# A channel gate behind a ConvNeXt block: two small layers as single-column products, or one product with a matrix of ones

## The chip, the cores and the metric

The kernel runs on one core of a Trainium2 chip. The metric is the device time of one execution in microseconds, from runs of the same program on a chip. The profile is of one further execution, so its own time is named wherever a sum is made from it. The engines are TensorE (PE in the profile, its weight loads PEld), VectorE (DVE), ScalarE (ACT), GpSimd (POOL) and SyncE (SP), whose queue here only starts transfers.

## What is computed

There are 32 samples of 384 channels and 28 x 28 places, all in f32. Layer 0 is a ConvNeXt block with a response normalization; layer 1 is a gate over channels, made from three statistics of each channel.

```python
# layer 0
y = conv7x7_depthwise(x)                       # per channel
y = (y - mean_c) * rsqrt(var_c + 1e-6)         # over channels, at each place
y = gelu(y @ w1 + b1)                          # 384 -> 1536
gx = sqrt(sum over places of y**2)
y = grn_g * (y * gx / (mean(gx) + 1e-6)) + grn_b + y
x = x + (y @ w2 + b2)                          # 1536 -> 384
# layer 1, R = 8
avg, mx, mn = mean, max, min of x over places  # each (32, 384)
avg_out = avg @ W1.T
max_out = einsum('brg,rg->br', mx.reshape(b, 8, 48), W2_1) * W2_2
min_out = mn @ W3.T
logits = concat([avg_out, max_out, min_out]) @ Wfc.T     # 24 -> 384
out = sigmoid(logits + x)
```

The last lines are the gate's two layers: 24 numbers a sample out of 3 x 384 statistics, and 384 logits out of the 24 numbers. A logit is added to every place of its channel.

## The kernel before

**Stage one (L175 to about L403).** The depthwise convolution of all samples runs as products with banded matrices. Four matrices (tmat, L203) are in flight; they are read from a table in DRAM that is built at the start from the filter weights (dww, L156). The input is loaded in 96 tiles (xi, L227), padded by GpSimd (xpad, L237), transposed by TensorE (pt, L248), and moved to SBUF by VectorE and ScalarE. There are 48 steps over the channels, eight a step (the loop at L315), each with three products a channel (L344, L345, L348). GpSimd also combines the weights of both dense layers in this stage (form_w, L268), because the dense layers use sums of blocks of weights, fewer products than the plain layer has; SyncE stores each combination (L277) in DRAM. The small constants are loaded in this stage too, one a step (the dictionary `later`).

**Stage two.** A loop over the samples runs up(b + 1), the first dense layer, and then down(b), the second. The rest of the work on other samples is hung between the steps of down as hooks (beside): the normalization of sample b + 2 (turn, stats, std), the forms of its input (forms_up, L542, ten GpSimd additions a sample), the scaling of sample b + 1 (grn and scale), and the gate of sample b - 1 (gate_store at hook 9, or hook 7 for the last). down has 15 steps of four products (L673) with 392 columns each. Each step's result is added to the residual x by VectorE (L687, L689). The last addition into a half of a channel block also sums it (accum_out into `sh`), and once both halves of a block are done VectorE takes its maximum and minimum over the places (L694, L695, into `st`). The operands of down are forms of y, made by GpSimd (forms, L648): seven are asked for at the last hook of the sample before (d_p, d_q, one in place, d_r, d_s, d_t, d_u) and three in down itself (d_v, and two written in place into y).

**The gate.** gate_store (from L701) runs 12 products of one column each into one bank: the six half sums, the three maxima and the three minima, each against a 128 x 24 matrix `gate` (L709). VectorE copies the 24 sums (comb, L714). Three products of one column with the 24 x 128 blocks of Wfc follow (pl, L717), and VectorE copies the logits (lg, L721). ScalarE adds them inside the sigmoid (L723), and its queue stores the sample (L729). The matrix `gate` is written between the stages in the code (L423 to L442).

**What sets the order.** The kernel is recorded by a layer that keeps tiles and their waits. It places each engine's instructions by when it reckons that they can run, so the order in an engine's queue need not be that of the code: the constants of the gate are written after stage one in the code, but their instructions stand in the queues among those of stage one. On an engine the queue runs in order. A pool with one buffer (psum `small`: pg, pa and pl share one bank) makes the next user wait for the last reader.

Of the kernel before, what the change touches and what calls it, by code (L numbers as in the profile page):

```python
# [8 lines left out]
F32 = mybir.dt.float32  # L9
AF = mybir.ActivationFunctionType  # L10
ALU = mybir.AluOpType
AX = mybir.AxisListType

P = 128
C = 384
CB = C // P
FF = 4 * C
FB = FF // P
HW = 28
NT = HW * HW  # L20
NH = NT // 2
RH = HW // 2
R = 8
EPS = 1e-6
# [95 lines left out]
def convnext_gate_kernel(  # L120
# [13 lines left out]
    nc = tc.nc  # L134
# [3 lines left out]
    const = ctx.enter_context(tc.tile_pool(name="const", bufs=1))  # L138
    dram = ctx.enter_context(tc.tile_pool(name="dram", bufs=1, space=bass.MemoryType.DRAM))
    smp = ctx.enter_context(tc.tile_pool(name="smp", bufs=3))  # L140
    pss = ctx.enter_context(tc.tile_pool(name="pss", bufs=1, space=bass.MemoryType.PSUM))

    def small(name):
        return pss.tile([P, 512], F32, tag="small", name=name)
# [7 lines left out]
    yl = dram.tile([P, NLAST, B, NJ * YC], F32, name="yl")  # L152


    dww = const.tile([P, CB, 49], F32, name="dww")
    nc.sync.dma_start(dww, dw_w.rearrange("(cb p) t -> p cb t", p=P))  # L156
    ident = const.tile([P, P], F32, name="ident")
    make_identity(nc, ident)
    cv = const.tile([P, 5, CB], F32, name="cv")
    _, lng_t, lnb_t, b2_t, w21_t = (cv[:, i, :] for i in range(5))  # L160
    fv = const.tile([P, 3, FB], F32, name="fv")
    b1_t, gg_t, gb_t = (fv[:, i, :] for i in range(3))
    ones_f = const.tile([P, P], F32, name="ones_f")
    nc.gpsimd.memset(ones_f, 1.0 / FF)
    awt = const.tile([P, 2, CB, R], F32, name="awt")
    w22b = const.tile([P, R], F32, name="w22b")
    wfc = const.tile([3 * R, C], F32, name="wfc")
    eps_t = const.tile([P, 1], F32, name="eps_t")
    nc.gpsimd.memset(eps_t, EPS)

# [4 lines left out]
    with ExitStack() as one:  # L175
        tp = one.enter_context(tc.tile_pool(name="tp", bufs=1))
# [5 lines left out]
        psc = one.enter_context(tc.tile_pool(name="psc", bufs=4, space=bass.MemoryType.PSUM))  # L182

        ws = tp.tile([P, CB * FF], F32, name="ws")
        tab = tp.tile([P, CB, FL], F32, name="tab")
        dwb = tp.tile([P, C], F32, name="dwb")


        NT2 = 4
# [74 lines left out]
        w1v = ws.rearrange("p (k t m c) -> p t k m c", t=KT, m=3, c=P)  # L264
        w2v = ws.rearrange("p (t k m c) -> p t k m c", t=KT, k=3, c=P)
        U1, U2 = 4, 22

        def form_w(name, wv, text, dst):  # L268

            t = ufp.tile([P, KT, P], F32, tag="uf", name=name)  # L270
            for n, (sg, m, k) in enumerate(terms(text)):
                blk = wv[:, :, int(k), m, :]
                if n == 0:
                    nc.gpsimd.tensor_scalar(t, blk, float(sg), None, ALU.mult)
                else:
                    nc.gpsimd.tensor_tensor(t, t, blk, ALU.add if sg > 0 else ALU.subtract)
            nc.sync.dma_start(dst, t)  # L277

        AHEAD = 6
        for i in range(AHEAD):  # L280
# [1 line left out]
        xt = new_xt(0)  # L282
# [32 lines left out]
        for s in range(NK):  # L315
# [8 lines left out]
            if s in later:  # L324

                dst, src = later[s]
# [11 lines left out]
            t = tmat[s % NT2]  # L338
# [56 lines left out]
                        nc.vector.bn_stats(bs0[:, j, 0, :], yi[:, : NY - NLAST, j, :])  # L395
            if si == SK - 1:
                xt = xn
            i = s - U1
            if 0 <= i < NS:
                form_w(f"u1_{i}", w1v, UPSTEPS[i][1], u1d[:, :, i, :].rearrange("t p c -> p t c"))  # L400
# [16 lines left out]

    def bank(name):
        return psz.tile([P, 512], F32, tag="pz", name=name)

    gate = const.tile([P, 3, CB, 3 * R], F32, name="gate")  # L423
    nc.vector.memset(gate, 0.0)
    nc.vector.tensor_scalar(gate[:, 0, :, 0:R], awt[:, 0], 1.0 / NT, None, ALU.mult)
    nc.vector.tensor_copy(gate[:, 2, :, 2 * R : 3 * R], awt[:, 1])
    grp = const.tile([P, CB, R], F32, name="grp")
    for cb in range(CB):
        nc.vector.tensor_scalar(grp[:, cb, :], w22b, w21_t[:, cb : cb + 1], None, ALU.mult)

    G = C // R
    grp_a = const.tile([P, CB, R], F32, name="grp_a")
    nc.gpsimd.affine_select(
        out=grp_a, in_=grp, pattern=[[P, CB], [-G, R]], compare_op=ALU.is_ge,
        fill=0.0, base=0, channel_multiplier=1,
    )
    grp_b = const.tile([P, CB, R], F32, name="grp_b")
    nc.gpsimd.affine_select(
        out=grp_b, in_=grp_a, pattern=[[-P, CB], [G, R]], compare_op=ALU.is_ge,
        fill=0.0, base=G - 1, channel_multiplier=-1,  # L440
    )
    nc.vector.tensor_copy(gate[:, 1, :, R : 2 * R], grp_b)  # L442


    x_tiles, yts, sts, accs, pts, feats = {}, {}, {}, {}, {}, {}
# [156 lines left out]
    def grn(b):  # L602

        ssq = ssqs.pop(b)
        gx = smp.tile([P, FB], F32, tag="gx", name=f"gx_{b}")
        nc.scalar.activation(gx, ssq, AF.Sqrt)
        gs = smp.tile([P, 1], F32, tag="gs", name=f"gs_{b}")
        nc.vector.tensor_reduce(gs, gx, AX.X, ALU.add)
        pg = small(f"pg_{b}")
        nc.tensor.matmul(pg[:, 0:1], ones_f, gs, start=True, stop=True)  # L610
        ge = smp.tile([P, 1], F32, tag="ge", name=f"ge_{b}")
        nc.vector.tensor_scalar(ge, pg[:, 0:1], EPS, None, ALU.add)
        gr = smp.tile([P, 1], F32, tag="gr", name=f"gr_{b}")
        nc.vector.reciprocal(gr, ge)
        gn = smp.tile([P, FB], F32, tag="gn", name=f"gn_{b}")
        nc.vector.scalar_tensor_tensor(gn, gx, gr, gg_t, ALU.mult, ALU.mult)
        gsc = gscs[b] = smp.tile([P, FB], F32, tag="gsc", name=f"gsc_{b}")
        nc.vector.tensor_scalar(gsc, gn, 1.0, None, ALU.add)  # L618
# [32 lines left out]
    def down(b, hooks):  # L651

        xt = x_tiles.pop(b)
        o = ops[b]
        st = smp.tile([P, 2, CB], F32, tag="st", name=f"st_{b}")
        sh = smp.tile([P, CB, 2], F32, tag="sh", name=f"sh_{b}")
        left = {}
        for step in STEPS:
            for _, m, h in terms(step[4]):
                left[m, h] = left.get((m, h), 0) + 1  # L660
        made = EARLY
        banks = {}
        for i, (opnd, _, bk, first, reads) in enumerate(STEPS):
            while opnd not in o:
                forms(b, made, made + 1)
                made += 1
            wt = up2.tile([P, KT, P], F32, tag="u2", name=f"u2_{b}_{i}")
            nc.sync.dma_start(wt.rearrange("p t c -> p (t c)"), u2d[i])
            if first:
                banks[bk] = bank(f"pz_{b}_{bk}")  # L670
            pz = banks[bk]
            for t in range(KT):
                nc.tensor.matmul(  # L673
                    pz[:, :NH],
                    wt[:, t, :],
                    o[opnd][:, t, :],
                    start=(first == 1 and t == 0),
                    stop=(t == KT - 1),
                    skip_group_check=True,
                )  # L680
            for sg, m, hn in terms(reads):
                h = "ab".index(hn)
                xh = xt[:, m, h * NH : (h + 1) * NH]
                op = ALU.add if sg > 0 else ALU.subtract
                left[m, hn] -= 1
                if left[m, hn]:
                    nc.vector.tensor_tensor(xh, xh, pz[:, :NH], op)  # L687
                    continue
                nc.vector.scalar_tensor_tensor(  # L689
                    xh, xh, b2_t[:, m : m + 1], pz[:, :NH], ALU.add, op,  # L690
                    accum_out=sh[:, m, h : h + 1],
                )
                if not left[m, "ab"[1 - h]]:
                    nc.vector.tensor_reduce(st[:, 0, m : m + 1], xt[:, m, :], AX.X, ALU.max)  # L694
                    nc.vector.tensor_reduce(st[:, 1, m : m + 1], xt[:, m, :], AX.X, ALU.min)  # L695
            run(hooks, i)
        ys.pop(b)
        ops.pop(b)
        gates[b] = xt, st, sh

    def gate_store(b):  # L701

        xt, st, sh = gates.pop(b)
        ov = out[b].rearrange("(cb p) n -> p cb n", p=P)
        pa = small(f"pa_{b}")
        cols = [(0, cb, sh[:, cb, h : h + 1]) for cb in range(CB) for h in range(2)]
        cols += [(v, cb, st[:, v - 1, cb : cb + 1]) for v in (1, 2) for cb in range(CB)]
        for n, (v, cb, col) in enumerate(cols):
            nc.tensor.matmul(  # L709
                pa[: 3 * R, 0:1], gate[:, v, cb, :], col,  # L710
                start=(n == 0), stop=(n == len(cols) - 1),
            )
        comb = smp.tile([3 * R, 1], F32, tag="comb", name=f"comb_{b}")
        nc.vector.tensor_copy(comb, pa[: 3 * R, 0:1])  # L714
        pl = small(f"pl_{b}")
        for cb in range(CB):
            nc.tensor.matmul(  # L717
                pl[:, cb : cb + 1], wfc[:, cb * P : (cb + 1) * P], comb, start=True, stop=True
            )
        lg = smp.tile([P, CB], F32, tag="lg", name=f"lg_{b}")  # L720
        nc.vector.tensor_copy(lg, pl[:, :CB])  # L721
        for cb in range(CB):
            nc.scalar.activation(  # L723
                xt[:, cb, :], xt[:, cb, :], AF.Sigmoid, bias=lg[:, cb : cb + 1], scale=1.0
            )
            if b == B - 1:
                nc.sync.dma_start(ov[:, cb, :], xt[:, cb, :])
        if b < B - 1:
            nc.scalar.dma_start(ov, xt)  # L729
# [138 lines left out]
```

## Time and profile before

| what | value |
|---|---|
| median of three runs | 3219.02 us (3218.94 to 3219.2) |
| the profiled execution, its own time | 3216.78 us |
| its span, first to last instruction | 3215.1 us, granted clock 0.996 |
| TensorE busy | 3174.8 us (99%) |
| VectorE, ScalarE, GpSimd busy | 1669.3, 1886.1, 1607.1 us |
| a sample in the steady stretch (pa to pa) | 84.19 us |
| end of stage one's last product | about 496.2 us |

The span is the time between the first and the last instruction of the profiled execution; 1.7 us of its own time lie around it. "Busy" means that an instruction of the engine was under way. A row of a timeline has the start in us, the duration in us, the engine, the line, the operation, the operands with their shapes, and the number of instructions merged into the row; a note in brackets gives the idle time of that engine just before and what ended it. One f32 product leaves two matmul records and two weight loads. A row of several merged products starts with the first and ends with the last, and since the products are pipelined, the distance from the start of one row to the start of the next is what a row costs.

### The profile page before, as it was taken

How to read it: one execution, taken by the hardware profiler on the slowest of the kernel's cores; microseconds unless marked ns; L12 is line 12 of the kernel's file. 1: busy time of each engine (PE TensorE's matmuls, PEld its weight loads, DVE VectorE, ACT ScalarE, POOL GpSimd, SP SyncE). 2: the span in 40 equal slices, each digit the busy share in tenths (PEclk: the TensorE clock that was granted, in tenths of full speed). 3: DMA queues.
4: the chain of work that ended last, by engine and by line, in shares of the span. 5: the costliest groups of instructions: out<-in, count | busy, mean ns of one | idle time of the engine just before them, and what ended most of it. 6: DMA issues, size and time to landing. Idle time of an engine off the chain costs nothing.

```text
span 3215.1 us, 35678 instructions
## 1 busy us (share of the span) xinstructions
PE 3174.8 (99%) x12352; PEld 2009.1 (62%) x12352; DVE 1669.3 (52%) x3442; ACT 1886.1 (59%) x3032; POOL 1607.1 (50%) x821
## 2 busy tenths in 40 slices
PE   8999998999999999999999999999999999999998
PEld 7999995555555555555555555555555555555555
DVE  3443436555555555555555555555555555555553
ACT  2222225766666666666666666666666666666662
POOL 2453511645555555555555555555555555555554
PEclk9999999999999999999999999999999999999999
DMA  9999985444444444344444444444444444444333
GB/s 346 364 340 359 341 296 183 131 131 136 130 139 143 141 141 139 132 136 143 134 142 145 134 145 143 136 140 139 146 146 129 137 129 141 142 141 141 125 101 126
DMA packets 257160, 540.84 MB, mean 168 GB/s; under 512 B 121021, under 2 KB 130774, under 8 KB 247766
## 3 DMA queue, kind: packets, MB, share of 16 engines
q1 hardware_dynamic: 244148, 500.70, 46.1%
q10 hardware_dynamic: 12834, 37.88, 3.5%
q8 instruction: 98, 1.61, 0.2%
q14 instruction: 80, 0.66, 0.1%
HBM read 447.53 MB, written 90.99 MB: 167 GB/s over the span
## 4 chain that ended last, share of the span: by engine, by line
PE 98%; DVE 1%; ACT 1%; DMA 1%; issue 0%; SPq 0%; ACTq 0%; POOL 0%; DVEq 0%; POOLq 0%
PE ph_A L576 14%; PE ph_B L576 13%; PE pz_A L673 11%; PE pz_B L673 10%; PE pz_C L673 5%; PE pz_E L673 5%; PE ph_C L576 5%; PE pc L344 5%; PE pc L345 4%; PE pc L348 4%; PE pz_F L673 3%; PE ph_D L576 3%; PE ph_H L576 3%; PE ph_F L576 3%; PE pz_G L673 3%; PE pz_D L673 3%
## 5 line engine op out<-in xcount | busy, mean ns | idle before, releaser
L648 POOL TENSOR_TENSOR d_v<-d_u,y 128x1568 f32<-128x1568 f32 x32 | 112.4, 3512 | 759.4 <-PE pz_B L673 735.4
L551 ACT ACTIVATE y<-y,fv 128x784 f32<-128x784 f32 x384 | 346.7, 941 | 214.5 <-DVE y L591 213.8
L484 ACT ACTIVATE y<-y,fv,gsc 128x784 f32<-128x784 f32 x378 | 358.6, 1027 | 30.1 <-DVE gsc L618 30.1
L557 ACT ACTIVATE junk<-y 128x784 f32<-128x784 f32 x384 | 326.7, 851 | 5.0
L648 POOL TENSOR_TENSOR d_p<-y 128x1568 f32<-128x1568 f32 x31 | 109.1, 3518 | 434.7 <-ACT y L484 434.7
L576 PE MATMUL ph_A<-af,u 128*128 128x392 f32 x768 | 313.7, 502 | 5.5 <-DVE af L542 5.4
L362 ACT ACTIVATE yc<-pc,dwb 128x224 f32<-128x224 f32 x192 | 103.8, 641 | 367.1 <-PE pc L348 264.4
L576 PE MATMUL ph_B<-af,u 128*128 128x392 f32 x768 | 311.3, 493 | 0.3 <-ACT y L583 0.3
L673 PE MATMUL pz_A<-y,u 128*128 128x392 f32 x768 | 268.8, 493 | 0.0
L648 POOL TENSOR_TENSOR y<-d_v,y 128x1568 f32<-128x1568 f32 x64 | 223.4, 3514 | 2.5
L576 PEld LDWEIGHTS ph_A<-af,u 128*128 128x128 f32 x768 | 136.4, 190 | 135.3 <-ACT y L583 57.8
L576 PE MATMUL ph_A<-acc,u 128*128 128x392 f32 x512 | 216.4, 504 | 0.0
L344 PE MATMUL pc<-xt,tmat 128*128 128x224 f32 x768 | 209.4, 354 | 6.7 <-issue 4.9
L576 PE MATMUL ph_B<-acc,u 128*128 128x392 f32 x512 | 213.6, 499 | 0.1
L576 PEld LDWEIGHTS ph_B<-af,u 128*128 128x128 f32 x768 | 145.2, 190 | 109.0 <-DVE y L587 9.6
L673 PEld LDWEIGHTS pz_A<-y,u 128*128 128x128 f32 x768 | 145.8, 190 | 106.4
L583 ACT ACTIVATE y<-ph_A 128x392 f32<-128x392 f32 x256 | 124.7, 487 | 145.0 <-PE ph_A L576 144.9
L237 POOL COPY xpad<-xi 128x784 f32<-128x784 f32 x96 | 80.6, 841 | 254.4 <-PE pt L248 188.1
L587 DVE TENSOR_TENSOR y<-y,ph_A 128x392 f32<-128x392 f32 x128 | 72.0, 563 | 238.9 <-PE ph_A L576 228.1
L473 ACT ACTIVATE sd<-mv,eps_t 128x7 f32<-128x7 f32 x32 | 9.6, 300 | 314.3 <-DVE mv L468 314.3
L542 POOL TENSOR_TENSOR af<-af,acc 128x392 f32<-128x392 f32 x186 | 187.2, 1020 | 4.9
L348 PE MATMUL pc<-xt,tmat 128*128 128x192 f32 x768 | 187.6, 326 | 0.0
(160 smaller groups left out, 7007.1 us busy)
## 6 DMA issues: line engine op xcount, KB each, us to landing
u<-u1d SPq DMA_DIRECT2D x128, 960.0 KB, 4.7
u<-u2d SPq DMA_DIRECT2D x480, 256.0 KB, 2.7
tmat<-fs SPq DMA_DIRECT2D x48, 1420.0 KB, 9.3
yd<-yc SPq DMA_DIRECT2D x22, 1792.0 KB, 8.4
yi<-yd SPq DMA_DIRECT2D x32, 1232.0 KB, 6.8
xi<-in_x SPq DMA_DIRECT2D x96, 392.0 KB, 9.4
x<-in_x SPq DMA_DIRECT2D x32, 1176.0 KB, 5.8
out<-x ACTq DMA_DIRECT2D x31, 1176.0 KB, 5.0
```

What stands on the lines that cost most here:

```text
L344: nc.tensor.matmul(pc[:, ci, :N], t[:, c, P : 2 * P], xc, start=True, stop=False)
L345: nc.tensor.matmul(pc[:REACH, ci, : N - B], t[:, c, 2 * P : T0 + MW], xc[:, B:], start=False, stop=False)
L348: nc.tensor.matmul(pc[:, ci, B:N], t[:, c, :P], xc[:, : N - B], start=False, stop=True)
L362: nc.scalar.activation(yc[:, :, :, cy + ci].rearrange("p b j -> p j b"), pc[:, ci, :N].rearrange("p (j b) -> p j b", j=NJ), AF.Identity, b ...
L484: eng.activation(out, in_, AF.Identity, bias=add, scale=mul)
L542: eng.tensor_tensor(d, o[in0], o[in1], op)
L551: nc.scalar.activation(y, y, AF.Gelu, bias=b1_t[:, f : f + 1], scale=1.0)
L557: nc.scalar.activation(junk, ys[b][:, f, :], AF.Square, accum_out=ssqs[b][:, f : f + 1])
L576: nc.tensor.matmul(banks[bk][:, :NH], wt[:, i, :], o[opnd], start=(first == 1), stop=True, skip_group_check=True,)
L583: nc.scalar.activation(d, p, AF.Identity)
L648: nc.gpsimd.tensor_tensor(d, o[in0], o[in1], op)
L673: nc.tensor.matmul(pz[:, :NH], wt[:, t, :], o[opnd][:, t, :], start=(first == 1 and t == 0), stop=(t == KT - 1), skip_group_check=True,)
```

## The change

The two layers of the gate become one product. A logit is a sum over all statistics and the eight numbers r of each kind:

    logit[c] = sum over q, r of fct[c, q, r] * (sum over channels p of gate[p, q, r] * st[p, q])

Here q counts 12 columns of statistics: three channel blocks of each half sum (six columns), three maxima, three minima. GpSimd multiplies `gate` (128 x 12 x 8) with the statistics, broadcast over r, into `zt`. One product of a 128 x 128 matrix of ones with zt's 96 columns sums over the channels and leaves the sums in every partition. VectorE multiplies them with `fct` (128 x 3 x 96, the transposed Wfc repeated over the columns of its kind) into `lt`, and a reduction over 96 gives the three logits of each partition. The matrix of ones was filled with 1/1536 for the mean in grn; it is 1 now, and grn's first VectorE instruction multiplies by 1/1536 instead, in the instruction that added EPS.

The constants gate and fct are written inside stage one, at step 40 in the code, with three transposes of Wfc on TensorE; dww, awt, w22b, wfc and the scratch for the groups move from the pool of constants to a pool of stage one. The store of a combined weight (form_w) is kept in a list and issued in the step after.

```diff
-    nc.gpsimd.memset(ones_f, 1.0 / FF)
+    nc.gpsimd.memset(ones_f, 1.0)
+    NQ = 4 * CB
+    gate = const.tile([P, NQ, R], F32, name="gate")
+    fct = const.tile([P, CB, NQ, R], F32, name="fct")
...
+        def gate_weights():
+            for h in range(2):
+                nc.vector.tensor_scalar(
+                    gate[:, : 2 * CB, :].rearrange("p (cb h) r -> p h cb r", h=2)[:, h],
+                    awt[:, 0], 1.0 / NT, None, ALU.mult,
+                )
+            nc.vector.tensor_copy(gate[:, 3 * CB :, :], awt[:, 1])
...
+            nc.gpsimd.affine_select(
+                out=grp_a, in_=grp, pattern=[[P, CB], [-G, R]], compare_op=ALU.is_ge,
+                fill=0.0, base=0, channel_multiplier=1,
+            )
+            nc.gpsimd.affine_select(
+                out=gate[:, 2 * CB : 3 * CB, :], in_=grp_a, pattern=[[-P, CB], [G, R]],
+                compare_op=ALU.is_ge, fill=0.0, base=G - 1, channel_multiplier=-1,
+            )
+            pf = small("pf")
+            for cb in range(CB):
+                nc.tensor.transpose(
+                    pf[:, cb * 3 * R : (cb + 1) * 3 * R], wfc[:, cb * P : (cb + 1) * P],
+                    ident[: 3 * R, : 3 * R],
+                )
+            for v in range(3):
+                q0, nq = ((0, 2 * CB), (2 * CB, CB), (3 * CB, CB))[v]
+                nc.vector.tensor_copy(
+                    fct[:, :, q0 : q0 + nq, :],
+                    pf[:, : CB * 3 * R]
+                    .rearrange("p (cb v r) -> p cb v r", cb=CB, v=3)[:, :, v, :]
+                    .unsqueeze(2)
+                    .to_broadcast([P, CB, nq, R]),
+                )
...
-            nc.sync.dma_start(dst, t)
+            stores.append((dst, t))
...
+            if s == SG:
+                gate_weights()
+            for dst, u in stores:
+                nc.sync.dma_start(dst, u)
+            stores.clear()
...
-        nc.vector.tensor_scalar(ge, pg[:, 0:1], EPS, None, ALU.add)
+        nc.vector.tensor_scalar(ge, pg[:, 0:1], 1.0 / FF, EPS, ALU.mult, ALU.add)
...
-                    accum_out=sh[:, m, h : h + 1],
+                    accum_out=st[:, 2 * m + h : 2 * m + h + 1],
...
+        n = NQ * R
+        zt = smp.tile([P, NQ, R], F32, tag="zt", name=f"zt_{b}", bufs=1)
+        nc.gpsimd.tensor_tensor(zt, gate, st.unsqueeze(2).to_broadcast([P, NQ, R]), ALU.mult)
         pa = small(f"pa_{b}")
-        for n, (v, cb, col) in enumerate(cols):
-            nc.tensor.matmul(
-                pa[: 3 * R, 0:1], gate[:, v, cb, :], col,
-                start=(n == 0), stop=(n == len(cols) - 1),
-            )
-        comb = smp.tile([3 * R, 1], F32, tag="comb", name=f"comb_{b}")
-        nc.vector.tensor_copy(comb, pa[: 3 * R, 0:1])
-        pl = small(f"pl_{b}")
-        for cb in range(CB):
-            nc.tensor.matmul(
-                pl[:, cb : cb + 1], wfc[:, cb * P : (cb + 1) * P], comb, start=True, stop=True
-            )
+        nc.tensor.matmul(
+            pa[:, :n], ones_f, zt.rearrange("p q r -> p (q r)"), start=True, stop=True
+        )
+        lt = smp.tile([P, CB, n], F32, tag="lt", name=f"lt_{b}", bufs=1)
+        nc.vector.tensor_tensor(
+            lt, fct.rearrange("p cb q r -> p cb (q r)"),
+            pa[:, :n].unsqueeze(1).to_broadcast([P, CB, n]), ALU.mult,
+        )
         lg = smp.tile([P, CB], F32, tag="lg", name=f"lg_{b}")
-        nc.vector.tensor_copy(lg, pl[:, :CB])
+        nc.vector.tensor_reduce(lg, lt, AX.X, ALU.add)
```

In the queues of the built program, the gate's product stands on TensorE where the twelve products stood (between the steps with d_u and d_v), and lt and lg stand on VectorE where comb and lg stood. The multiplication into zt for sample 0 stands among the forms of sample 1. From sample 1 to sample 29, zt of sample b stands behind the forms_up additions that are made during down(b), and ahead of d_p of sample b + 1.

More of the change, by code (lines that the diff above doesn't have):

```diff
@@ L152, in convnext_gate_kernel @@
     yl = dram.tile([P, NLAST, B, NJ * YC], F32, name="yl")
-    dww = const.tile([P, CB, 49], F32, name="dww")
-    nc.sync.dma_start(dww, dw_w.rearrange("(cb p) t -> p cb t", p=P))
     ident = const.tile([P, P], F32, name="ident")
@@ L163, in convnext_gate_kernel @@
     ones_f = const.tile([P, P], F32, name="ones_f")
-    nc.gpsimd.memset(ones_f, 1.0 / FF)
-    awt = const.tile([P, 2, CB, R], F32, name="awt")
-    w22b = const.tile([P, R], F32, name="w22b")
-    wfc = const.tile([3 * R, C], F32, name="wfc")
+    nc.gpsimd.memset(ones_f, 1.0)
+    NQ = 4 * CB
+    gate = const.tile([P, NQ, R], F32, name="gate")
+    fct = const.tile([P, CB, NQ, R], F32, name="fct")
     eps_t = const.tile([P, 1], F32, name="eps_t")
@@ L184, in convnext_gate_kernel @@
         ws = tp.tile([P, CB * FF], F32, name="ws")
+        dww = tp.tile([P, CB, 49], F32, name="dww")
+        nc.sync.dma_start(dww, dw_w.rearrange("(cb p) t -> p cb t", p=P))
         tab = tp.tile([P, CB, FL], F32, name="tab")
         dwb = tp.tile([P, C], F32, name="dwb")
+        awt = tp.tile([P, 2, CB, R], F32, name="awt")
+        w22b = tp.tile([P, R], F32, name="w22b")
+        wfc = tp.tile([3 * R, C], F32, name="wfc")
+        grp = tp.tile([P, CB, R], F32, name="grp")
+        grp_a = tp.tile([P, CB, R], F32, name="grp_a")
         NT2 = 4
@@ L266, in convnext_gate_kernel @@
         U1, U2 = 4, 22
+        stores = []
+        SG = 40
+        def gate_weights():
[6 more added lines that the diff above has]
+            for cb in range(CB):
+                nc.vector.tensor_scalar(
+                    grp[:, cb, :], w22b, w21_t[:, cb : cb + 1], None, ALU.mult
+                )
+            G = C // R
+            nc.gpsimd.affine_select(
[7 more added lines that the diff above has]
+            pf = small("pf")
+            for cb in range(CB):
+                nc.tensor.transpose(
[11 more added lines that the diff above has]
+                )
         def form_w(name, wv, text, dst):
@@ L419, in bank @@
         return psz.tile([P, 512], F32, tag="pz", name=name)
[L423 to L427, printed above, removed]
-    for cb in range(CB):
[L429 to L435, printed above, removed]
-    )
[L437 to L440, printed above, removed]
-    )
-    nc.vector.tensor_copy(gate[:, 1, :, R : 2 * R], grp_b)
     x_tiles, yts, sts, accs, pts, feats = {}, {}, {}, {}, {}, {}
@@ L654, in down @@
         o = ops[b]
-        st = smp.tile([P, 2, CB], F32, tag="st", name=f"st_{b}")
-        sh = smp.tile([P, CB, 2], F32, tag="sh", name=f"sh_{b}")
+        st = smp.tile([P, NQ], F32, tag="st", name=f"st_{b}")
         left = {}
@@ L690, in down @@
                     xh, xh, b2_t[:, m : m + 1], pz[:, :NH], ALU.add, op,
-                    accum_out=sh[:, m, h : h + 1],
+                    accum_out=st[:, 2 * m + h : 2 * m + h + 1],
                 )
                 if not left[m, "ab"[1 - h]]:
-                    nc.vector.tensor_reduce(st[:, 0, m : m + 1], xt[:, m, :], AX.X, ALU.max)
-                    nc.vector.tensor_reduce(st[:, 1, m : m + 1], xt[:, m, :], AX.X, ALU.min)
+                    for v, op2 in ((2, ALU.max), (3, ALU.min)):
+                        q = v * CB + m
+                        nc.vector.tensor_reduce(st[:, q : q + 1], xt[:, m, :], AX.X, op2)
             run(hooks, i)
@@ L698, in down @@
         ops.pop(b)
-        gates[b] = xt, st, sh
+        gates[b] = xt, st
     def gate_store(b):
-        xt, st, sh = gates.pop(b)
+        xt, st = gates.pop(b)
         ov = out[b].rearrange("(cb p) n -> p cb n", p=P)
+        n = NQ * R
+        zt = smp.tile([P, NQ, R], F32, tag="zt", name=f"zt_{b}", bufs=1)
+        nc.gpsimd.tensor_tensor(zt, gate, st.unsqueeze(2).to_broadcast([P, NQ, R]), ALU.mult)
         pa = small(f"pa_{b}")
-        cols = [(0, cb, sh[:, cb, h : h + 1]) for cb in range(CB) for h in range(2)]
-        cols += [(v, cb, st[:, v - 1, cb : cb + 1]) for v in (1, 2) for cb in range(CB)]
-        for n, (v, cb, col) in enumerate(cols):
-            nc.tensor.matmul(
-                pa[: 3 * R, 0:1], gate[:, v, cb, :], col,
-                start=(n == 0), stop=(n == len(cols) - 1),
-            )
-        comb = smp.tile([3 * R, 1], F32, tag="comb", name=f"comb_{b}")
-        nc.vector.tensor_copy(comb, pa[: 3 * R, 0:1])
-        pl = small(f"pl_{b}")
-        for cb in range(CB):
-            nc.tensor.matmul(
-                pl[:, cb : cb + 1], wfc[:, cb * P : (cb + 1) * P], comb, start=True, stop=True
-            )
+        nc.tensor.matmul(
[5 more added lines that the diff above has]
+            pa[:, :n].unsqueeze(1).to_broadcast([P, CB, n]), ALU.mult,
+        )
         lg = smp.tile([P, CB], F32, tag="lg", name=f"lg_{b}")
-        nc.vector.tensor_copy(lg, pl[:, :CB])
+        nc.vector.tensor_reduce(lg, lt, AX.X, ALU.add)
         for cb in range(CB):
```

## The prediction

> **What bounds the kernel now.** I read the page first: the busy times and the chain of work that ended last.
>
> ```profile
> PE 3174.8 (99%) x12352; PEld 2009.1 (62%) x12352; DVE 1669.3 (52%) x3442; ACT 1886.1 (59%) x3032; POOL 1607.1 (50%) x821
> ...
> PE 98%; DVE 1%; ACT 1%; DMA 1%; issue 0%; SPq 0%; ACTq 0%; POOL 0%; DVEq 0%; POOLq 0%
> ```
>
> TensorE is busy in 99% of the span and carries 98% of the last chain; every other engine idles about half of the time. So a microsecond taken out of TensorE's queue shortens the run, unless TensorE then waits for somebody. Next the timeline of TensorE around the gate of one sample, in the steady stretch (start, us, engine, line, operation, operands, count).
>
> ```profile
> 1375.91 2.80 PE L673 MATMUL pz_A<-y,u 128*128 128x392 f32 x8
> 1378.54 0.28 PE L610 MATMUL pg<-gs,ones_f 128*128 128x1 f32 x2
> 1378.68 2.88 PE L673 MATMUL pz_C<-d_u,u 128*128 128x392 f32 x8
> 1381.49 0.46 PE L709 MATMUL pa<-sh,gate 128*24 128x1 f32 x12
> 1381.81 0.44 PE L709 MATMUL pa<-st,gate 128*24 128x1 f32 x12
> 1382.18 0.93 PE L673 MATMUL pz_A<-d_v,u 128*128 128x392 f32 x2
> 1383.04 0.82 PE L717 MATMUL pl<-comb,wfc 24*128 24x1 f32 x6
> 1383.79 2.24 PE L673 MATMUL pz_A<-d_v,u 128*128 128x392 f32 x6
> 1385.87 2.80 PE L673 MATMUL pz_F<-y,u 128*128 128x392 f32 x8
> ```
>
> Each product leaves two records[...]. The gate's 15 small products stand in the middle of the second layer's stream, and nothing runs beside them on TensorE. Sample 0 is the control: the same steps, without a gate, since there is no sample before it.
>
> ```profile
> 620.13 2.80 PE L673 MATMUL pz_A<-y,u 128*128 128x392 f32 x8
> 622.77 0.28 PE L610 MATMUL pg<-gs,ones_f 128*128 128x1 f32 x2
> 622.91 2.88 PE L673 MATMUL pz_C<-d_u,u 128*128 128x392 f32 x8
> 625.62 2.80 PE L673 MATMUL pz_A<-d_v,u 128*128 128x392 f32 x8
> 628.26 2.80 PE L673 MATMUL pz_F<-y,u 128*128 128x392 f32 x8
> ```
>
> From the start of pz_A to the start of pz_F it is 8.13 us without a gate (628.26 - 620.13) and 9.96 us with one (1385.87 - 1375.91). The gate costs **1.83 us of TensorE a sample**. It stands so 31 times, at hook 9 of samples 1 to 30 and hook 7 of sample 31; the last gate, after the last step, is a tail. Last, GpSimd's queue, which gets a new instruction.
>
> ```profile
> 1377.57 5.17 POOL L542 TENSOR_TENSOR af<-af,acc 128x392 f32<-128x392 f32 x5
> 1396.22 3.54 POOL L648 TENSOR_TENSOR d_p<-y 128x1568 f32<-128x1568 f32 x1 [13.47 <-ACT y L484]
> ...
> 1417.51 3.52 POOL L648 TENSOR_TENSOR d_u<-d_t,y 128x1568 f32<-128x1568 f32 x1
> 1446.26 3.51 POOL L648 TENSOR_TENSOR d_v<-d_u,y 128x1568 f32<-128x1568 f32 x1 [25.23 <-PE pz_B L673]
> ```
>
> Its forms for up (af) end at 1382.74, 1.25 us after TensorE reached pa; then it idles 13.5 us, and 25.2 us more after d_u.
>
> [...]a weight load costs by its columns, not its rows. [...]98 to 103 ns for pa's 128x24, but 181 to 187 ns for pl's 24x128, about as much as a full 128x128 (190). So pl's three products pay full loads for 24 rows. [...]The trace: (3514 - 1020) ns over 1568 - 392 elements is 2.12 ns an element, and 0.19 us fixed. [...]the trace's 128x392 took 0.56 us[...].
>
> **The change part by part.**
>
> *Taken off TensorE:* 12 pa and 3 pl products, 31 times 1.83 us = 56.7 us.
>
> *Put on TensorE:* one product, ones_f (128x128) with 96 columns. The nearest row is pg: the same matrix with one column. It costs 8.13 less three steps of 2.635 (pz_A to pz_F rows, 628.26 - 625.62 = 2.64; 8 records) = 0.23 us, which is weight loads. 96 columns stream in 96/392 of 0.329 us = 0.08 us a record, less than the load of 0.12 beside it (pl: six records in 0.75), so I take 0.23. Bounds: 0.16 (two times 0.08, all loads hidden) and 0.43 (0.23 and an uncovered first load; pl started 0.20 us after the product ahead of it ended, 1382.18 + 0.66 to 1383.04). Its wait is for ge, which frees the bank at 1379.44, 2 us before TensorE gets there, so I expect cover. Gain **1.60 us a sample** (1.40 to 1.67), times 31 = 49.6 us (43.4 to 51.8).
>
> *zt on GpSimd:* 0.19 + 96 x 2.12 ns = 0.39 us. Were it queued behind the af of the same turn, TensorE would wait. In the order of the built program it isn't: from sample 1 on, zt of sample b stands behind the af formed in down(b) and ahead of d_p of b+1, a turn (about 65 us) before pa of b. What it waits for there is the last minimum of sample b, which ends at 1399.12. So d_p and the six forms behind it, which began at 1396.22, begin near 1399.6, 3.4 us later. Cover: d_u then ends at 1424.4, and d_v waits for TensorE until 1446.26; d_p is read by TensorE at 1443.3. The zt of sample 30 stands between d_v and x of sample 31, where x ends at 3175.1 and TensorE wants it at 3183.7. Cost 0; if the delay passed some 20 us it would cost one for one. A gain is excluded, since TensorE's step is set elsewhere.
>
> *lt and lg on VectorE:* 288 elements from PSUM[...], and a reduction of as many, from the row 128x784 at 0.97 us, about 0.45. They replace two copies (0.15 and 0.16). VectorE stands idle 2.0 us before pz_A's evacuation at 1386.07, which will come 1.6 us earlier; lt starts after the evacuation of pz_C (1381.60 + 0.56), so lg is ready near 1383.1. ScalarE's sigmoid starts at 1385.13, after a table load that doesn't wait. Cost 0.
>
> *ScalarE's slack:* it scales y until 1396.14, counted from pg; TensorE's first ph_A, 1396.40 now, comes at 1394.80, and its evacuation would be due at 1395.66. ScalarE is 0.5 us late. Cover: the next product into bank A comes 3.95 us after the first (1312.22, 1316.17), and ScalarE gains 0.16 us with each evacuation. Cost 0; uncovered, 0.5 a sample.
>
> *Constants:* the selects and gate weights stood in the first stage's queues already (grp_a at 129.9), so nothing leaves the seam between stages, and the waits of the second stage's first loads stay the same in the built program. New are three transposes of wfc, at most pt's 0.22 us each, 0.7 us, and three VectorE copies in its idle time. Their wait is for wfc, issued at 116.0; TensorE gets there near 143 (with the 33rd padded tile, 138.0), and small loads landed in up to 14.3 us. Bound of a loss: 0 to 1.
>
> *Stores of the combined weights, and dww:* each store is issued a step later, on SP past the next tmat. SP waited 127.7 us in all for GpSimd at these stores. But TensorE waited for no tmat or other load in the first 520 us, and was busy 394 of the 400 us from 80 to 480. Cost 0, bounds -2.2 (four of five 80 us stretches raised to the best) and +3 (a late load now and then). A buffer is asked for again a step (9.76 us, 130.10 to 139.86 in the transposes) after the later store, which lands in 5.2. dww only changes its pool.
>
> *Tail:* the last minimum ends at 3206.71, and the sigmoid started at 3208.27, 1.56 us later. New: wake 0.05, zt 0.39, one product with its loads in the open 0.45, wake 0.06, lt 0.46, lg 0.45 and wakes 0.1: 1.96 to 2.1. Cost +0.5 (0.2 to 1.0).
>
> *Sum:* -49.6 + 0.7 + 0.5 = **-48.4 us**. The profiled execution took 3216.78 us (span 3215.1, 1.7 around it), so 3168.4 for such a one; the median of the runs, 2.24 us above it, goes from 3219.02 to **3170.6**.
>
> **Rivals.** *An uncovered load:* pa's first weight load isn't drawn ahead, as with pl and pa now (pz_C to pa is 0.10 longer than pz_C to pz_A in the control). Against it: pg loads ahead with the same matrix. Then 31 x 1.40 = 43.4, less 1.2: 3176.8. *ScalarE in the way:* each of 29 starts of up is 0.46 us late: 3170.6 + 13.3 = 3183.9. Against it: 2 us of cover in bank A. *GpSimd in the way (slower):* the product becomes ready only after the af of its own turn. Then TensorE waits from 1381.4 to 1382.74 + 0.39 + a wake of 0.05 = 1.78 us, and the load is uncovered too, 0.43: 2.21 against 1.83, 29 times 0.38 = +11, less 3.2 for the two samples without af, and 1.2: 3228. It decides once zt ends over 1.6 us after pz_C. For it: the code issues zt at hook 9. Against it: the built order, by a whole turn. *The constants do it, not the products:* no; they were in the first stage before.
>
> **How the numbers follow.** Forecast 82%, uncovered load 9%, ScalarE 5%, GpSimd 2%, something in the first stage outside its bounds 2%. Range: low end 51.8 + 2.2 gained, with 0.7 and 0.2 lost: 3165.9, taken as 3166; high end 43.4, less 0.7, 1.0 and 3: 3180.3, taken as 3180. It takes in the uncovered load, not the ScalarE and GpSimd cases. A measurement of this kernel can tell about 0.2%, 6.4 us, from no change. All cases but GpSimd's, and half of the 2%, end faster by more: 0.97; within, 0.01; slower, 0.02.
>
> **What would show it.** Right: a pa row 128x96 with 64 records; pz_A to pz_F 8.36 us; the period 84.19 down to 82.59; zt near 0.39 us and d_p 3.4 us later against TensorE; d_v still released by pz_B; the first stage's end within 2 us of before. Wrong: TensorE idle before pa, released by POOL zt; ph_A released by ScalarE; d_v no longer released by pz_B; or a later end of the first stage.

## The result, and the profile after

| | before | after |
|---|---|---|
| median of four runs each, on one chip | 3218.98 us (3217.48 to 3219.2) | 3167.85 us (3166.88 to 3168.3) |
| the profiled execution, its own time | 3216.78 us | 3168.3 us |
| its span | 3215.1 us | 3166.6 us |
| median of a sample's period (pg to pg) | 84.19 us | 82.57 us |
| pz_A to pz_F around the gate | 9.96 us | 8.35 us |

The ratio is 0.9844, with a 95% interval from 0.9832 to 0.9855: 51 us faster, and the forecast of 3170.6 lies 2.8 us above the median. A repetition in another group of runs gave 3167.96 us against 3218.1 (0.9844, 0.9829 to 0.9858).

The busy times and the chain of work that ended last, of the kernel after:

```profile
PE 3125.4 (99%) x11459; PEld 1978.5 (62%) x11459; DVE 1685.1 (53%) x3444; ACT 1878.7 (59%) x3032; POOL 1616.9 (51%) x853
...
PE 98%; DVE 1%; ACT 1%; DMA 1%; issue 0%; ACTq 0%; POOL 0%; POOLq 0%; SPq 0%; DVEq 0%
```

TensorE is still 99% busy and still carries 98% of the chain, but it has 893 matmul records fewer and is busy 49.4 us less. VectorE has gained 15.8 us of work and GpSimd 9.8, both far from full. The work was moved from the engine that bounds the kernel to two that don't.

TensorE's timeline around the gate of one sample, after (start, us, engine, line, operation, operands, count):

```profile
1365.14 2.80 PE L703 MATMUL pz_A<-y,u 128*128 128x392 f32 x8
1367.78 0.28 PE L641 MATMUL pg<-gs,ones_f 128*128 128x1 f32 x2
1367.92 2.88 PE L703 MATMUL pz_C<-d_u,u 128*128 128x392 f32 x8
1370.63 0.36 PE L740 MATMUL pa<-zt,ones_f 128*128 128x96 f32 x2
1370.83 2.83 PE L703 MATMUL pz_A<-d_v,u 128*128 128x392 f32 x8
1373.49 2.80 PE L703 MATMUL pz_F<-y,u 128*128 128x392 f32 x8
```

Three rows of small products have become the one row pa. Read the starts, not the durations: from pz_A to pz_F it is 8.35 us (1373.49 - 1365.14). Sample 0, which has no gate, still takes 8.12, so the gate costs 0.22 to 0.23 us of TensorE instead of 1.83.

GpSimd's queue in the same stretch, after:

```profile
1366.80 5.18 POOL L573 TENSOR_TENSOR af<-af,acc 128x392 f32<-128x392 f32 x5
1386.88 0.35 POOL L738 TENSOR_TENSOR zt<-gate,st 128x96 f32<-128x96 f32 x1 [14.90 <-DVE st L726]
1387.19 3.53 POOL L679 TENSOR_TENSOR d_p<-y 128x1568 f32<-128x1568 f32 x1
...
1408.47 3.53 POOL L679 TENSOR_TENSOR d_u<-d_t,y 128x1568 f32<-128x1568 f32 x1
1433.87 3.51 POOL L679 TENSOR_TENSOR d_v<-d_u,y 128x1568 f32<-128x1568 f32 x1 [21.87 <-PE pz_B L703]
```

zt waits for VectorE's last minimum and d_p stands behind it: ScalarE has the last of y at 1385.39 (a row of 1377.84 and 7.55), and d_p begins at 1387.19, after zt. The delay is gone by d_v, which still waits 21.87 us for TensorE (25.23 before). So zt runs a turn ahead of its product: the zt made at 1386.88 is read by the pa at 1453.21, a period after the pa row above.

The end of the run, all engines, after:

```profile
3152.81 2.80 PE L703 MATMUL pz_A<-y,u 128*128 128x392 f32 x8
...
3158.32 0.35 POOL L738 TENSOR_TENSOR zt<-gate,st 128x96 f32<-128x96 f32 x1 [24.84 <-DVE st L726]
...
3158.73 0.46 PE L740 MATMUL pa<-zt,ones_f 128*128 128x96 f32 x2 [3.12 <-POOL zt L738]
3159.23 0.46 DVE L744 TENSOR_TENSOR lt<-fct,pa 128x288 f32<-128x288 f32 x1 [1.07 <-PE pa L740]
3159.72 0.45 DVE L749 TENSOR_REDUCE lg<-lt 128x3 f32<-128x288 f32 x1
3160.20 2.62 ACT L751 ACTIVATE x<-x,lg 128x784 f32<-128x784 f32 x3 [13.88 <-DVE lg L749]
```

Here the chain of the new gate is in the open: statistics, zt, pa, lt, lg, sigmoid, each released by the one before.

### The profile page after: what moved, and what is told of

It reads as the page before. It is cut to its first block, busy times and chain, and to the rows that moved or that the text cites. A ratio compares the mean times of both kernels' runs of the same rounds, so it can differ in the third digit from the quotient of the medians.

```text
span 3166.6 us, 33843 instructions
## 1 busy us (share of the span) xinstructions
PE 3125.4 (99%) x11459; PEld 1978.5 (62%) x11459; DVE 1685.1 (53%) x3444; ACT 1878.7 (59%) x3032; POOL 1616.9 (51%) x853
## 4 chain that ended last, share of the span: by engine, by line
PE 98%; DVE 1%; ACT 1%; DMA 1%; issue 0%; ACTq 0%; POOL 0%; POOLq 0%; SPq 0%; DVEq 0%
PE ph_A L607 14%; PE ph_B L607 13%; PE pz_A L703 11%; PE pz_B L703 11%; PE pz_C L703 5%; PE ph_C L607 5%; PE pz_E L703 5%; PE pc L393 5%; PE pc L394 4%; PE pc L397 4%; PE pz_F L703 3%; PE ph_D L607 3%; PE ph_H L607 3%; PE ph_F L607 3%; PE pz_G L703 3%; PE pz_D L703 3%
## 5 line engine op out<-in xcount | busy, mean ns | idle before, releaser
L738 POOL TENSOR_TENSOR zt<-gate,st 128x96 f32<-128x96 f32 x32 | 11.2, 350 | 456.9 <-DVE st L726 456.9
```

## The experiments

**The kernel before once more, and the stores.** In the profiled execution the first product of stage two (ph_A) came at 510.34 us before and at 512.46 after. If the change did that, 2.1 us of gain were lost in stage one, and the repetition of the kernel after, with its first ph_A at 512.16, seems to say so. Two runs ask further: the kernel before once more, and the kernel after with the stores of the combined weights issued at once.

```diff
-            stores.append((dst, t))
+            nc.sync.dma_start(dst, t)
```

> The kernel before once more, for the scatter of its first stage: the first products of up started at 510.3 us. Scatter of single executions: another start within 2 us of that. If the first stage is the same to 0.3 us in every execution: 510.3 again, and the 512.5 of the changed kernel belongs to the change.

> The changed kernel with each store of a combined weight issued at once, as in the kernel before. If the later stores cost nothing and save nothing (my prediction): 3168, and the first products of up at the same place to 1 us. If they cost the 2.1 us that the first stage grew: 3166. If they save SyncE waits that matter: 3170 or more.

The kernel before had its first ph_A at 511.85 this time, and its first pg at 570.62 (568.41 in its first profile), where the kernel after has 570.62 too. With stores at once: ph_A at 511.08, and 3168.19 us (3166.95 to 3169.09; ratio 0.9846, 0.9833 to 0.9859), no different from after. In the eight other runs below that keep stage one as it is in the kernel after, the first ph_A came from 510.43 to 512.72. So the start of stage two varies by some 2 us between executions, a loss in stage one can't be told from that, and the delayed stores neither cost nor save anything that can be measured.

**What the product's 0.22 us are made of.** The prediction took them for two weight loads that the 96 columns hide behind. If so, one column costs as much, and columns that outlast the loads cost more. The first edit leaves one column, the second streams the 96 four times.

```diff
-            pa[:, :n], ones_f, zt.rearrange("p q r -> p (q r)"), start=True, stop=True
+            pa[:, :1], ones_f, zt.rearrange("p q r -> p (q r)")[:, :1], start=True, stop=True
...
-            pa[:, :n].unsqueeze(1).to_broadcast([P, CB, n]), ALU.mult,
+            pa[:, :1].unsqueeze(1).to_broadcast([P, CB, n]), ALU.mult,
```

```diff
-            pa[:, :n], ones_f, zt.rearrange("p q r -> p (q r)"), start=True, stop=True
+            pa[:, : 4 * n].rearrange("p (k q) -> p k q", k=4), ones_f,
+            zt.rearrange("p q r -> p (q r)").unsqueeze(1).to_broadcast([P, 4, n]),
+            start=True, stop=True,
```

> The product with the matrix of ones has one column instead of 96; the sums of the other 95 columns are left out (the multiplication behind it reads the one column 96 times). Theory: the product's 0.22 us in the stream are its two weight loads, so columns are free up to about the length of a load: 8.35 us from pz_A to pz_F as before this edit, time 3168 within 2 us of the changed kernel. Rival: the columns cost (96 of 392 of two passes is 0.16 us a product): 31 times 0.16 = 5 us faster, 3163.

> The product streams zt's 96 columns four times, 384 columns in all, of which the same 96 are read. Theory: now the columns outlast the two loads; a product of 392 columns costs 2.635 / 4 = 0.66 us in the stream, so 384 cost 0.645 instead of 0.22: pz_A to pz_F 8.77 us, 31 times 0.43 = 13 us slower than the changed kernel, 3181. Rival: a product among those of 392 columns costs what its place costs, whatever its width: 3168.

With one column: 3168.1 us (3166.91 to 3168.94; ratio 0.9846, 0.9832 to 0.9859) and 8.35 us from pz_A to pz_F. With 384 columns: 3181.36 us (3180.38 to 3182.21; ratio 0.9886, 0.9873 to 0.99). TensorE's timeline with 384 columns:

```profile
1368.43 2.80 PE L703 MATMUL pz_A<-y,u 128*128 128x392 f32 x8
1371.07 0.28 PE L641 MATMUL pg<-gs,ones_f 128*128 128x1 f32 x2
1371.20 2.88 PE L703 MATMUL pz_C<-d_u,u 128*128 128x392 f32 x8
1373.92 0.81 PE L740 MATMUL pa<-zt,ones_f 128*128 128x384 f32 x2
1374.57 2.80 PE L703 MATMUL pz_A<-d_v,u 128*128 128x392 f32 x8
1377.20 2.80 PE L703 MATMUL pz_F<-y,u 128*128 128x392 f32 x8
```

pz_A to pz_F is now 8.77 us: 8.12 and 0.65, what 384 columns cost in the stream of large products. Both are the theory's numbers, and both rivals fall. Of these three widths, 1 and 96 columns cost the same and 384 cost their columns.

**No product of its own at all.** The mean in grn (pg) is a sum over channels with the same matrix of ones, 2.9 us earlier. For 29 of the gates the 96 columns can ride with that sum's one: at the mean of sample b, the gate of sample b - 2 is due (`products` is the GpSimd multiplication as in the kernel after, made into the first 96 columns).

```diff
-        nc.tensor.matmul(pg[:, 0:1], ones_f, gs, start=True, stop=True)
...
+        if 3 <= b + 1 <= B - 1:
+            zt = smp.tile([P, n + 1], F32, tag="zt", name=f"zg_{b}", bufs=1)
+            products(b - 2, zt[:, :n].rearrange("p (q r) -> p q r", r=R))
+            nc.vector.tensor_reduce(zt[:, n : n + 1], gx, AX.X, ALU.add)
+            nc.tensor.matmul(pg[:, : n + 1], ones_f, zt, start=True, stop=True)
+            sums[b - 2] = pg
...
```

> The sum for grn and the gate's sums as one product of 97 columns at the place of pg, in the 29 samples where both stand in down; the rest as before. My theory: a product of so few columns costs its two weight loads and nothing for its columns, so the 97 columns cost what pg alone did, 0.22 us, and the product of its own goes: 29 x 0.22 = 6.4 us less, 3161.5. The rival, that columns are paid beside the loads (0.16 us for 96), expects 1.7 us less, 3166. A second rival: the joint product makes lt wait in front of grn's VectorE steps, so that the scaling comes late and the gain is lost, 3168.

3161.63 us (3160.57 to 3162.87), ratio 0.9824 (0.9809 to 0.9838): the fastest version here, 6.2 us below the kernel after. Its timeline on TensorE:

```profile
1363.45 2.80 PE L719 MATMUL pz_A<-y,u 128*128 128x392 f32 x8
1366.08 0.36 PE L650 MATMUL pg<-zg,ones_f 128*128 128x97 f32 x2
1366.28 2.82 PE L719 MATMUL pz_C<-d_u,u 128*128 128x392 f32 x8
1368.94 2.80 PE L719 MATMUL pz_A<-d_v,u 128*128 128x392 f32 x8
1371.57 2.80 PE L719 MATMUL pz_F<-y,u 128*128 128x392 f32 x8
```

8.12 us, what sample 0 takes without a gate. The period fell from 82.57 to 82.36; 29 x 0.21 is the 6 us.

**The rival that ends slower, made true.** In the kernel after, zt stands a turn ahead of its product. Here a term made from a form of its own turn (times zero, so the value stays) is added to the statistics, which puts zt behind the forms for up.

```diff
+        if b + 3 < B:
+            sx = smp.tile([P, 1], F32, tag="sx", name=f"sx_{b}", bufs=1)
+            nc.gpsimd.tensor_scalar(sx, feats[b + 3]["z"][:, 0:1], 0.0, None, ALU.mult)
+            su = smp.tile([P, NQ], F32, tag="su", name=f"su_{b}", bufs=1)
+            nc.gpsimd.tensor_tensor(su, st, sx.to_broadcast([P, NQ]), ALU.add)
+            st = su
```

> zt is made to depend on the last af of its own turn (two small GpSimd instructions more, which add zero times one of its values), so it can only be queued behind them. My theory: TensorE then stands before pa until zt is there: af ends 1.35 us after pa's place, then about 0.19 + 0.21 + 0.35 us and two or three wakes, 2.2 to 2.5 us a sample in 29 samples: 3232 to 3240, slower than the kernel before, with POOL zt as the releaser of pa. If the place of zt on GpSimd doesn't matter, 3168.

3248.44 us (3247.19 to 3248.95), ratio 1.0093 (1.0076 to 1.0109): slower than before, and 8 us above the range. TensorE's waits, its first line:

```profile
PE pa L746 <- POOL zt L744: 68.2, 30, 3.1
```

Its cause in GpSimd's timeline, and the effect in TensorE's, in the same kernel:

```profile
1387.53 5.16 POOL L573 TENSOR_TENSOR af<-af,acc 128x392 f32<-128x392 f32 x5
1392.78 0.21 POOL L740 TENSOR_SCALAR sx<-af 128x1 f32<-128x1 f32 x1
1393.07 0.21 POOL L742 TENSOR_TENSOR su<-st,sx 128x12 f32<-128x12 f32 x1
1393.36 0.35 POOL L744 TENSOR_TENSOR zt<-gate,su 128x96 f32<-128x96 f32 x1
```

```profile
1388.64 2.88 PE L703 MATMUL pz_C<-d_u,u 128*128 128x392 f32 x8
1393.77 0.46 PE L746 MATMUL pa<-zt,ones_f 128*128 128x96 f32 x2 [2.24 <-POOL zt L744]
1394.06 2.83 PE L703 MATMUL pz_A<-d_v,u 128*128 128x392 f32 x8
```

The product waits 2.24 us, and the rest is, by the author's estimate, its first load, no longer hidden (one 128x128 load takes 0.19 us in the kernel after): pz_A to pz_F is 10.86 us (1396.73 - 1385.87), 2.51 more than in the kernel after and 0.90 more than before. Of the 0.90 the two helping instructions take 0.58 (two of 0.29, 1392.78 to 1393.36). The remaining 0.32 stands beside the 0.38 that the prediction gave this rival. So the mechanism is real and about its size.

The distance is 10.83 to 10.88 us in 24 of the 29 samples, and 12.42 to 12.53 in the other five. One of the five:

```profile
881.70 0.74 PE L746 MATMUL pa<-zt,ones_f 128*128 128x96 f32 x2 [2.23 <-POOL zt L744]
882.24 4.17 PE L703 MATMUL pz_A<-d_v,u 128*128 128x392 f32 x8
```

The wait is the same, but the eight records after it took 4.17 us instead of 2.83, at a granted clock of 0.52 (mean of 881.7 to 885.1 us). Five times 1.6 us are the 8 us above the range; the expectation had no such term, nor had the prediction's sum for this rival.

So the product gains 51 us with zt a turn ahead in GpSimd's queue, and this version loses 30. Of these 30, about 17 (29 x 0.58) are the two helping instructions.

**How much cover GpSimd has.** zt is computed 40 times and 110 times in samples 0 to 29.

```diff
-        nc.gpsimd.tensor_tensor(zt, gate, st.unsqueeze(2).to_broadcast([P, NQ, R]), ALU.mult)
+        for _ in range(40 if b < B - 2 else 1):
+            nc.gpsimd.tensor_tensor(zt, gate, st.unsqueeze(2).to_broadcast([P, NQ, R]), ALU.mult)
```

> zt is computed 40 times over on GpSimd (the same values): 39 x 0.31 to 0.35 us, 12 to 14 us more a sample ahead of d_v, in 30 samples. My theory: GpSimd's idle time before d_v (21.9 us) takes all of it: 3168, no idle TensorE. The rival, that the later forms are paid at once, expects 12 us a sample, 3500.

> zt computed 110 times over: 109 x 0.31 to 0.35 = 34 to 38 us more ahead of d_v. My theory: 21.9 us of idle time and some 6.7 us of slack between x's form and its product take 28.6, and the rest is paid by TensorE, one for one, before the step with x (pz_A from y): 5 to 9.5 us a sample in some 29 samples, 3310 to 3440. If only the idle time covers it: 12 to 16 us a sample, 3520 to 3640. If GpSimd's queue has no bearing: 3168.

40 times: 3167.73 us (3167.62 to 3169.01; ratio 0.9845, 0.9831 to 0.9858), no cost; d_v's wait for TensorE shrank from 21.87 to 5.95 us. 110 times: 3759.25 us (ratio 1.1682, 1.1661 to 1.1703), far above the range. The sign was right and the size wrong. Of TensorE's waits, GpSimd's timeline and TensorE's timeline with 110, the lines that say why:

```profile
PE pz_A L703 <- POOL y L679: 495.6, 30, 17.1
```

```profile
1383.09 41.53 POOL L739 TENSOR_TENSOR zt<-gate,st 128x96 f32<-128x96 f32 x97
1424.57 3.48 POOL L679 TENSOR_TENSOR d_v<-d_u,y 128x1568 f32<-128x1568 f32 x1
```

```profile
1431.67 5.41 PE L703 MATMUL pz_A<-y,u 128*128 128x392 f32 x8 [17.06 <-POOL y L679]
```

97 multiplications took 41.53 us, 0.43 each, not the 0.35 of one alone. The 109 more are then about 46 us a sample (97 of the 110 stand here, the others earlier in the queue). Of these, 21.9 were d_v's idle time and 6.75 the time between the form y that follows d_v (ended at 1440.97 in the kernel after) and the pz_A that reads it (1447.72). The rest, about 17.4, is the wait, measured 17.06. And the eight records after it took 5.41 us instead of 2.80, because the granted clock had fallen to 0.52 (mean of 1431.6 to 1437.0 us). 17.06 and 2.6 make 19.7 of the 19.8 us by which the period grew.

**zt on VectorE.**

```diff
-        nc.gpsimd.tensor_tensor(zt, gate, st.unsqueeze(2).to_broadcast([P, NQ, R]), ALU.mult)
+        nc.vector.tensor_tensor(zt, gate, st.unsqueeze(2).to_broadcast([P, NQ, R]), ALU.mult)
```

> The multiplication into zt goes to VectorE instead of GpSimd. Theory: the sums are ready a turn ahead either way and both engines are off the path; zt stands on VectorE behind the last minimum of its sample and costs about 0.25 us there, d_p on GpSimd comes 3.4 us earlier again, and nobody waits for either: 3168 within 2 us of the changed kernel. Rival: VectorE is late at the start of the next up, where it has to evacuate the first banks, and TensorE waits about 0.3 us in each of 29 samples: 3177.

3169.52 us (3168.57 to 3170.28), ratio 0.985 (0.9836 to 0.9863). The period stayed at 82.57, as the theory had it; once in the run TensorE waited 1.4 us for a VectorE result at a start of up, the rival's place, but not in each of 29 samples. The price of zt was missed by a factor of nine. VectorE's and GpSimd's timelines at one zt:

```profile
1385.85 1.84 DVE L726 TENSOR_REDUCE st<-x 128x1 f32<-128x784 f32 x2
1387.73 2.32 DVE L738 TENSOR_TENSOR zt<-gate,st 128x96 f32<-128x96 f32 x1
1390.55 0.56 DVE L618 TENSOR_TENSOR y<-y,ph_A 128x392 f32<-128x392 f32 x1 [0.50 <-PE ph_A L607]
```

```profile
1386.41 3.53 POOL L679 TENSOR_TENSOR d_p<-y 128x1568 f32<-128x1568 f32 x1 [13.47 <-ACT y L515]
1389.89 3.53 POOL L679 TENSOR_TENSOR d_q<-y 128x1568 f32<-128x1568 f32 x1
```

zt ends at 1390.05, 0.11 us after d_p does (1389.94). In 31 of the 32 samples zt ends 0.10 to 0.13 us after the GpSimd instruction that was under way; only the last zt, with GpSimd idle, took 0.26 us.

**The gate without its sum over channels.**

```diff
-        pa = small(f"pa_{b}")
-        nc.tensor.matmul(
-            pa[:, :n], ones_f, zt.rearrange("p q r -> p (q r)"), start=True, stop=True
-        )
+        pa = zt.rearrange("p q r -> p (q r)")
```

> The one product with the matrix of ones is left out: lt reads zt itself, so the sum over the channels is missing from the output. My theory: the product costs TensorE 0.22 us a sample, so pz_A to pz_F falls from 8.35 to 8.13 us as in sample 0, and the time by 31 x 0.22 = 7 us, with some 0.4 us less in the tail: 3160.5. The rival, that the product is already hidden under its neighbours, expects 3168 and no change in that distance.

3685.88 us, ratio 1.1452 (1.1435 to 1.1469). The distance did what the theory said: pz_A to pz_F is 8.12 us in all 30 samples that have these two rows, so sample 0 was a fair control. The time missed, and it doesn't measure pa: without the product the recording layer placed lt a turn ahead in VectorE's queue, in the middle of up, and zt behind d_t on GpSimd. All engines around one lt, in this kernel:

```profile
1352.10 0.35 POOL L738 TENSOR_TENSOR zt<-gate,st 128x96 f32<-128x96 f32 x1
1352.41 3.48 POOL L679 TENSOR_TENSOR d_u<-d_t,y 128x1568 f32<-128x1568 f32 x1
1352.49 3.72 DVE L741 TENSOR_TENSOR lt<-fct,zt 128x288 f32<-128x288 f32 x1 [14.37 <-POOL zt L738]
1356.13 0.55 DVE L620 TENSOR_TENSOR te<-ph_B,te 128x392 f32<-128x392 f32 x1
...
1356.74 1.02 PE L607 MATMUL ph_B<-acc,u 128*128 128x392 f32 x1 [16.60 <-DVE te L620]
```

VectorE stands still for 14.37 us before lt, te is queued behind it, and TensorE waits 16.60 us for the bank that te frees. Over the run TensorE waited 454 us at ph_B in 30 such places (334.5 and 120.0 by releaser), of the 518 us by which this kernel is slower than the kernel after. The cost of pa is settled by the distance, the two widths and the merged product.

## Why the prediction was right

**Products taken off and put on.** Forecast 1.60 us a sample, measured 1.61 (9.96 - 8.35); pa 0.23, measured 0.22 to 0.23; the period 82.59, measured 82.57. That 96 columns add nothing was inferred from pg's row; one column, 384 columns and the merge now show it. That the weight loads set the floor is supported by the kernel before, in the prediction's lines: with one column each, a product with a 24-column weight took 0.06 us (twelve pa in 0.69, 1381.49 to 1382.18), one with a 128-column weight 0.25 (three pl in 0.75). The rival of an uncovered load didn't come in the stream: TensorE has no wait at pa but that of the tail (3.1 us, once), and pa's first load begins at 1370.31, 0.32 us ahead of its product. The prediction mixed up two hooks (the gate of sample 29, in sample 30's down, stands at hook 7, the others in a down at hook 9); its count of 31 is not touched.

**zt on GpSimd.** 0.39 forecast, from GpSimd's own rows of before (2.12 ns an element), 0.35 measured. d_p against TensorE's first ph_A: 0.18 us ahead before (1396.22, 1396.40), 3.17 behind after (1387.19, 1384.02), 3.35 later where 3.4 was forecast. Cost 0, and 40 of them cost 0 too. The bound "some 20 us" was short: by the profile after it is 21.9 + 6.75, about 28.6 us, and the wait with 110 multiplications fits that. Nor is it one for one beyond the bound: the clock after the wait cost 2.6 us a sample more.

**lt and lg.** 0.46 and 0.45 forecast, 0.447 and 0.453 measured (means of 32). The 0.46 for lt was the author's figure, shown by no row of before. VectorE's rows there (0.56 us for 128x392, 0.97 for 128x784) put 288 elements at 0.45, an estimate along a straight line through two different operations. In the kernel after, nothing waits for them in the stream.

**ScalarE's slack.** ScalarE reaches ph_A's evacuation 1.27 us after TensorE's ph_A starts (1385.29, 1384.02), against 0.86 before: 0.41 late, forecast 0.5. By the next ph_A it is 0.86 behind again (1388.83, 1387.97). TensorE has no wait for it at ph_A.

**Constants and stores.** Forecast +0.7 and 0. No loss can be told apart: the start of stage two varies by more in the kernel before itself (510.34, 511.85). That moving the constants alone costs nothing was not tried by itself.

**Tail.** From the start of the last pz_A to the sigmoid 6.91 us before (3201.36, 3208.27), 7.39 after (3152.81, 3160.20): +0.48, forecast +0.5. To the end of the span it is only +0.1 (13.7 and 13.8): the last of the output's stores was issued 2.6 us after the sigmoid's start before and 2.7 after (3210.9, 3162.9), and the span ended 4.2 and 3.7 us behind that.

**The sum.** The two profiled executions differ by 48.48 us, and the forecast said 48.4. That closeness is partly luck: the profiled execution of before had an early stage two. Against the second profile of before, whose first pg came at the same time as after's, the last product of down ended 50.67 us sooner (3206.28, 3155.61): 31 x 1.61 = 49.9, and two periods of before that were 0.25 us longer than the others. The medians differ by 51.1, so the forecast's small losses (0.7 and 0.5) can't be seen in the whole.

## What to carry to other kernels

Where one engine is full, count what a small product costs by the distance of its neighbours' starts, with an instance that lacks it as control: here 15 one-column products were 1.83 us and one 96-column product 0.23, where 96 columns were free and 384 were not. A second small sum with the same stationary matrix belongs in the same product (another 6 us). What made this safe was the place of the feeding instruction in the other engine's queue, a turn ahead. Look it up in the built order: a version that held it back a turn lost 30 us where this one gains 51, though 17 of the 30 were the instructions that held it back.

## What the runs showed of the hardware that was not expected

**Two VectorE instructions ended only after GpSimd's.** zt on VectorE took 2.32 us instead of 0.26, and lt 3.72 us in the run without the sum (1352.49 to 1356.21, with d_u on GpSimd from 1352.41 to 1355.89) instead of 0.447 where it reads PSUM. Both have two operands in SBUF; two reductions beside the same GpSimd work, with one each, kept their 1.84 us. The GpSimd instruction had started first each time, and zt ended 0.11 us after it, lt 0.32. In the kernel after, lt takes one operand from PSUM, and in 29 of its 32 times it ran beside GpSimd's af (1371.32 to 1371.76, af from 1370.97 to 1371.99) and kept its 0.447 us. What makes the one instruction end after the other these runs don't show.

**The same GpSimd instruction repeated into one tile** came every 0.43 us, where one took 0.35 and the next instruction, into another tile, started 0.31 after it (1386.88, 1387.19). That each repeat waits for the end of the one before would explain it, but was not tried. An estimate of a repeated cost needs the distance of starts too.

**TensorE's clock after a wait.** After 17.06 us of idle time the granted clock was 0.52 over the next 5.4 us, and eight records took 5.41 us instead of 2.80. So this wait, which comes once a sample, cost 2.6 us more than itself. Of the 29 waits of about 2.2 us with zt in its own turn, five cost 1.6 us more than the other 24; in the one shown above the clock was 0.52 over 3.4 us. What decides between them stays open.
